# Graph attention on one core: forward maxima kept in PSUM, column numbers in bf16 beside the sums, and a new place for ScalarE's comparison

## The chip, the cores and the metric

The kernel runs on 1 core of a Trainium2 chip. The engines of the core are TensorE (PE; its weight loads are shown as PEld), VectorE (DVE), ScalarE (ACT), GpSimd (POOL) and SyncE (SP). Each runs its own queue of instructions in order and waits for the others by semaphores. The metric is the device time of the whole kernel in microseconds (us); lower is better. Several runs are taken and their median is given. One further execution is recorded by the profiler, and all durations of single instructions come from it.

## The reference

A graph has 6250 nodes with 128 features and 200,000 edges, sorted by their destination `dst`. After a layer norm and a ReLU come two edge convolutions and one attention layer. Only the attention is touched by the change:

```python
q = (h @ qw + qb).reshape(n, H, HD)          # H = 8 heads of HD = 16
k = (h @ kw + kb).reshape(n, H, HD)
v = (h @ vw + vb).reshape(n, H, HD)
logits = (q[dst] * k[src]).sum(-1) * scale + (edge_attr @ ew + eb)
amax = jax.ops.segment_max(logits, dst, num_segments=n)
pe = jnp.exp(logits - amax[dst])
ssum = jax.ops.segment_sum(pe, dst, num_segments=n)
w = pe / jnp.clip(ssum[dst], 1e-06)
o = jax.ops.segment_sum(w[:, :, None] * v[src], dst, num_segments=n)
```

The convolutions ahead of it gather rows of `src` in the same way, put them through a small network for each edge and sum by `dst`.

## The kernel before

**Tiling.** The edges are cut into 196 chunks of 1024 (NT = 8 columns of 128 edges). As they are sorted by destination, a chunk's destinations nearly always lie in a narrow window of nodes, and its sums go to two neighbouring blocks of 128 nodes of a table in SBUF (`flat`). What does not fit into a window is done later in loops (`leftovers`, `left`, `left_rows`).

**Stages.** `conv(1)`, `conv(2)` and the attention each run `pipeline`, which writes out the instructions step by step: step n fetches chunk n + 2 (GpSimd gathers its rows from memory in eight indirect DMAs, L618; SyncE loads the rest), computes the first half for chunk n and the second half for some earlier chunk. `in_order` then fixes this written order for VectorE, ScalarE, TensorE and SyncE. So where a line stands in `pipeline` decides where it stands in its engine's queue. GpSimd's gathers wait for free buffers.

**One step of the attention, in the order of the code.**

- `compared` (L613, L614; ScalarE): turns the relative destinations of chunk n + 2 into a matrix of zeros and ones, `ohT`, by a square and a ReLU. It works in place on 112 x 1024 values.
- `second`, for a chunk k about nine steps old, whose maxima are known: `onehot` (L624, VectorE) compares the column numbers `iota` with each edge's destination to give `oh`; `add_late` (L1261 to L1267, VectorE) adds the rescaled sums of chunk k-2 to the table; `weighted` has ScalarE fill a column of `v` with the weights `pe` (L1234) and VectorE multiply the gathered values by them (L1235); ScalarE fills two more pieces of `v` (L1340, L1341); `sums` (L1242, TensorE) multiplies `oh` by `v` in eight accumulating products (two passes each, so 16 in the profile) into a PSUM tile `u`; `merge_late` (L1275, L1278, L1249 to L1257) takes the maxima of chunk k-1 from its `u`, compares them with those kept so far (VectorE) and computes two rescaling factors by exponentials, `al` (L1255, written back into `u`) and `be` (L1257) (ScalarE).
- `first`, that is `logits`, for chunk n: VectorE multiplies the products `qe` by the gathered keys in two pieces (L1178: banks 0 and 1 of `qe`, then bank 2), ScalarE copies the edge terms `ebs` out of `qe` after each (L1179), and VectorE reduces and adds (L1181, L1183).
- `products` (L1169, TensorE) makes `qe` for chunk n + 1.
- One piece of a batch of finished nodes (`attention_nodes`).

**Maxima by runs.** For a run of up to eight chunks, `maxima` finds the maximum of each destination. TensorE transposes the logits `lg` into PSUM, so that 64 rows (8 chunks x 8 heads) hold the 1024 edges in order, in two halves of 512, which share one PSUM buffer (tag `blk`). VectorE scans each half forward into `fw` in SBUF (L1210), and then scans `fw` backward in place (L1213); `nbs` and `nbe` reset the maximum where a destination begins and ends. TensorE transposes the result back into `rm`. There are 23 runs of eight and then runs of 6, 4 and 2. `maxima` is a generator whose pieces are woven into `second`.

**PSUM.** Eight banks of 512 f32 per partition: `iota` one, `blk` one (also used by the node batches), `qe` three, `pe` one, and `u` two, one for each of two rotating buffers. The tile framework sets the semaphore waits from what each instruction reads and writes.

Of the kernel before, what the change touches and what calls it, by code (L numbers as in the profile page):

```python
# [8 lines left out]
FP = mybir.dt.float32  # L9
BF = mybir.dt.bfloat16  # L10
I32 = mybir.dt.int32
AF = mybir.ActivationFunctionType
ALU = mybir.AluOpType
# [8 lines left out]
P = 128  # L22
D = 128
H = 8
HD = 16
NT = 8
CH = NT * P
G = 8
# [16 lines left out]
def kernel(ctx: ExitStack, tc: tile.TileContext, x, src, dst, eat, w, out):  # L45
# [621 lines left out]
                nc.sync.dma_start(out=k.ea, in_=eat[:, bass.ds(c * CH, CH)])  # L667
                body(k)

    def left_rows(k, pools, rows_d, tag, shape, bufs):  # L670

        lp = pools["left"]
        k.rows = lp.tile([P, DB], FP, name="l_rows")
        nc.vector.memset(k.rows[:, D:], 0.0)
        nc.sync.dma_start(out=k.rows[:, :D], in_=rows_d[bass.ds(k.win * P, P), :])
        onehot(k, pools, iota_j)
        k.ohf = lp.tile([P, NT, P], FP, name="l_ohf")
        per = shape[1]
        for a in range(0, NT, per):
            n = min(per, NT - a)  # L680
            tp = pools["ps"].tile(shape, FP, name="l_tp", tag=tag, bufs=bufs)
            for t in range(n):
                nc.tensor.transpose(tp[:, t, :P], k.oh[:, a + t, :], ident)
            nc.scalar.copy(k.ohf[:, a:a + n, :], tp[:, :n, :P])
# [13 lines left out]
    def pipeline(i, stage, aside=iter(())):  # L698

        start = len(nc.cur_bb.bb.instructions)
        ends, todo = steps_of(i)
        starts = {n: j for j, (n, _) in enumerate(plans[i])}
        ahead = stage.ahead
        ks, under_way = {}, []
        for c in range(ahead):  # L710
            ks[c] = stage.fetch(c)
            compared(ks[c])
        stage.products(ks[0])
        for n, seconds in enumerate(todo):
            if n + ahead < NCH:
                ks[n + ahead] = stage.fetch(n + ahead)
            if n + 1 < NCH and stage.soon:
                stage.products(ks[n + 1])
            run = [ks[c] for c in ends.get(n, ())]
            stage.root(run)  # L720
            if n + ahead < NCH:
                compared(ks[n + ahead])
            stage.second(run, [ks.pop(c) for c in seconds])
            if n < NCH:
                stage.first(ks[n])
            stage.finish()
            if n + 1 < NCH and not stage.soon:
                stage.products(ks[n + 1])
            if n + 1 < len(todo) and todo[n + 1]:
                stage.early(ks[todo[n + 1][0]])  # L730
            if n in starts:
                for _ in aside:
                    pass
                under_way.append(stage.batch(starts[n]))
            for g in list(under_way):
                if next(g, STOP) is STOP:
                    under_way.remove(g)
            if n > 4:
                next(aside, None)
            if n < NCH:  # L740
                stage.reduce(ks[n])
        stage.flush()
        for g in (*under_way, aside):
            for _ in g:
                pass
        in_order(start)
# [205 lines left out]
    def conv(i):  # L952
# [4 lines left out]
        with ExitStack() as es:  # L957
# [154 lines left out]
            nc.sync.dma_start(out=wcl, in_=wc_d[i])  # L1112

            def left(k):
                left_rows(k, pools, a_d[i], "m", [P, NT, D], 2)
                k.g = gp.tile([P, NT, D], FP, name="g")
                gather(k, k.g, b_d[i])
                k.h = hs[0]
                hidden(k, [(k.ohf.rearrange("p t e -> p (t e)"), k.rows[:, :D]), (k.ea, wcl)])
                var = vp.tile([P, NV + BN * H], FP, name="var")  # L1120
                first(k, var, 0)()
                nc.vector.reciprocal(rs_ps[:, :NT * H], deviations(NT * H, var)[:, :NT * H])
                k.rs = rs_ps[:, :NT * H]
                normed(k)
                summed(k)
                s = U[:, bass.ds(k.win, 1), :wide].rearrange("p o c -> p (o c)")
                nc.vector.tensor_tensor(s, s, k.u[:, 0, :wide], ALU.add)
# [23 lines left out]
    with ExitStack() as es:  # L1151
# [1 line left out]
        pools = {"oh": pool("oh", 2), "ps": pool("ps", 1, space=PSUM)}  # L1153
        gp, wk, vp = pool("gp", G + 3), pool("wk", 2), pool("vp", 1)
        ps_ = pools["ps"]
        iota = ps_.tile([P, D], FP, name="iota")
        nc.vector.tensor_copy(iota, iota_j)
        nodes = Nodes(np_of(pool("np", 1)), lambda: ps_.tile([P, BN, D], FP, name="nd", tag="blk"))

        TB = 3  # L1160
        WHOLE = NT // TB
# [34 lines left out]
        def maxima(run, lg, nb, bp):  # L1196

            n, c0 = len(run), run[0].c  # L1200
            q = n * H
            fw = bp.tile([G * H, CH], FP, name="fw")
            half = CH // 2
            for a in range(2):
                lt = ps_.tile([G * H, 4, P], FP, name="lt", tag="blk")
                for t in range(4):
                    nc.tensor.transpose(lt[:q, t, :], lg[:, 4 * a + t, :n, :].rearrange("p c h -> p (c h)"), ident)
                yield
                at = slice(a * half, (a + 1) * half)
                nc.vector.tensor_tensor_scan(  # L1210
                    fw[:q, at], nb["nbs"][:q, at], lt[:q].rearrange("p t e -> p (t e)"),
                    fw[:q, half - 1:half] if a else -BIG, ALU.add, ALU.max)
            nc.vector.tensor_tensor_scan(  # L1213
                fw[:q, ::-1], nb["nbe"][:q, ::-1], fw[:q, ::-1], -BIG, ALU.add, ALU.max)
            rm = ps_.tile([P, NT, G, H], FP, name="rm", tag="blk")
            for t in range(NT):
                nc.tensor.transpose(rm[:, t, :n, :].rearrange("p c h -> p (c h)"), fw[:q, t * P:(t + 1) * P], ident[:q, :q])
            yield
            wl = vp.tile([P, NT, G, H], FP, name="wl")
            e3 = ef[:, c0 * NT:(c0 + n) * NT].rearrange("p (c t) -> p t c", t=NT)  # L1220
            nc.vector.tensor_tensor(lg[:, :, :n, :], lg[:, :, :n, :], rm[:, :, :n, :], ALU.subtract)
            pe = ps_.tile([P, NT, G, H], FP, name="pe", tag="pe")
            nc.scalar.activation(pe[:, :, :n, :], lg[:, :, :n, :], AF.Exp)
            for t in range(NT):
                nc.vector.tensor_tensor(
                    wl[:, t, :n, :], rm[:, t, :n, :], e3[:, t, :, None].to_broadcast([P, n, H]), ALU.mult)
            for j, k in enumerate(run):
                k.pe, k.wl = pe[:, :, j, :], wl[:, :, j, :]
# [8 lines left out]
                k.pe[:, :, :, None].to_broadcast([P, NT, H, HD]), ALU.mult)  # L1237

        def sums(k, wide):
            k.u = ps_.tile([P, 512], FP, name="u", tag="u", bufs=2)  # L1240
            for t in range(NT):
                nc.tensor.matmul(k.u[:, :wide], lhsT=k.oh[:, t, :], rhs=k.v[:, t, :wide],  # L1242
                                 start=(t == 0), stop=(t == NT - 1))

        def merge(k, m, tt, cm, n):


            mn = wk.tile([P, n, H], FP, name="mn")
            nc.vector.tensor_tensor(mn, cm, m, ALU.max)  # L1249
            d = wk.tile([P, 2, n, H], FP, name="d")  # L1250
            nc.vector.tensor_tensor(d[:, 0], m, mn, ALU.subtract)
            nc.vector.tensor_tensor(d[:, 1], cm, mn, ALU.subtract)  # L1252
            nc.vector.tensor_copy(m, mn)
            k.al = k.u[:, 160:160 + n * H].rearrange("p (q h) -> p q h", h=H)
            nc.scalar.activation(k.al, d[:, 0], AF.Exp)  # L1255
            k.be = wk.tile([P, n, H], FP, name="be")
            nc.scalar.activation(k.be, d[:, 1], AF.Exp)  # L1257

        def add(k, tt, n):
            tt = tt.rearrange("p q (h c) -> p q h c", c=HD + 1)  # L1260
            nc.vector.tensor_tensor(tt, tt, k.al[:, :, :, None].to_broadcast([P, n, H, HD + 1]), ALU.mult)  # L1261
            up = k.u[:, 192:192 + n * VK].rearrange("p (q h c) -> p q h c", h=H, c=HD + 1)
            u = k.u[:, :VK].rearrange("p (h c) -> p h c", c=HD + 1)
            for q in range(n):
                nc.vector.tensor_tensor(
                    up[:, q], u, k.be[:, q, :, None].to_broadcast([P, H, HD + 1]), ALU.mult)
            nc.vector.tensor_tensor(tt, tt, up, ALU.add)  # L1267
# [17 lines left out]
        class Stage:  # L1285
# [34 lines left out]
            def second(self, run, ks):  # L1320
# [6 lines left out]
                for n, k in enumerate(ks):  # L1327
                    mine = pieces if n == len(ks) - 1 else iter(())
                    next(mine, None)
                    onehot(k, pools, iota)  # L1330
                    if self.sums:
                        self.sums[0].win = value(w0_i, self.sums[0].c, DVE, NW - 1)
                    next(mine, None)
# [37 lines left out]

        def left(k):
            lp = pools["left"]
            left_rows(k, pools, a_d[3], "blk", [P, BN, P], 1)
            k.g = gp.tile([P, NT, KV], FP, name="g")
            gather(k, k.g, kv_d)
            products(k, [(k.ohf.rearrange("p t e -> p (t e)"), k.rows), (k.ea, webl)])
# [5 lines left out]
            for a in range(2):  # L1383
                nc.vector.tensor_scalar(neg, k.ohf[:, 4 * a:4 * a + 4, :], 1.0, BIG, ALU.subtract, ALU.mult)
                for h in range(H):
                    bc = ps_.tile([P, 4, P], FP, name="l_bc", tag="blk")
                    for t in range(4):
                        nc.tensor.transpose(bc[:, t, :], lg[:, 4 * a + t, h:h + 1].to_broadcast([P, P]), ident)
                    nc.vector.tensor_tensor_reduce(
# [59 lines left out]
```

## Time and profile before

| | |
|---|---|
| time, median of 3 runs | 6209.37 us (6209.28 to 6218.48) |
| the profiled execution | 6216.17 us, of which the span of instructions is 6214.2 us |
| VectorE busy | 5103.6 us (82%) |
| GpSimd busy | 4541.8 us (73%) |
| TensorE matmuls busy | 3590.1 us (58%) |
| ScalarE busy | 3301.8 us (53%) |
| TensorE's granted clock, mean | 0.769 |

The two convolutions take the first 4,100 us or so (the first gather of the attention starts at 4110.62 us), the attention and its last nodes the rest. In a row of a group stand the line, the engine, the operation, the output and the inputs, the shape and the count; then the busy time in us and the mean in ns; then the idle time of the engine just before these instructions, and which instruction or transfer ended it. In a timeline row stand the start, the duration, the engine and the line, and in brackets the idle time ahead. The durations of neighbours on one engine may overlap by some hundredths of a microsecond. GpSimd's 0.30 us between two gathers is its time for issuing and not a wait for others. The names of tiles come without their numbers. The clock is the share of the full rate that TensorE was granted: a busy TensorE at a low clock works more slowly.

### The profile page before, as it was taken

Reading aid. Unit: us, or ns where it says so; the run is one execution under the profiler, and the core shown is the slowest. Engines: PE = TensorE matmul, PEld = TensorE weight load, DVE = VectorE, ACT = ScalarE, POOL = GpSimd, SP = SyncE. Lnnn points to the kernel's source line nnn. Section 1 sums busy time; section 2 is a strip of 40 time slices with the busy share of each in tenths; the row PEclk is TensorE's granted clock in tenths of the full one; section 3 lists DMA queues with packets and bytes.
Section 4 is the critical chain, followed back from the end, with each engine's and each line's share of the span. In section 5 each row is a group of like instructions: output and inputs, shape, how many; then the busy total and the mean of one; then the engine's idle time right before and its main releaser. Section 6 shows DMA issues by size and latency. Waiting matters only on the chain. (4 is left out here: it accounts for less than half of the span.)

```text
span 6214.2 us, 71765 instructions
## 1 busy us (share of the span) xinstructions
PE 3590.1 (58%) x20957; PEld 3411.2 (55%) x20958; DVE 5103.6 (82%) x7368; ACT 3301.8 (53%) x5097; POOL 4541.8 (73%) x4718
## 2 busy tenths in 40 slices
PE   4555555555555455555655565645665566565655
PEld 4555555555555455555655555635555555555554
DVE  6878888888888677877888888847788888888888
ACT  5666666666666566666666666633333333333332
POOL 5777777777777577777777777757777777777773
PEclk8777777777877777777787778767777877887787
DMA  6544444444444344444444444445666666666653
GB/s 166 127 111 110 102 125 111 108 115 114 109 114 108 88 108 108 104 107 109 116 113 122 122 121 118 113 116 157 162 163 167 169 167 164 172 171 165 171 160 75
DMA packets 414303, 800.30 MB, mean 129 GB/s; under 512 B 101813, under 2 KB 274984, under 8 KB 379496
## 3 DMA queue, kind: packets, MB, share of 16 engines
q0 software_dynamic: 175616, 411.34, 27.4%
q1 hardware_dynamic: 232646, 380.69, 22.3%
q10 hardware_dynamic: 5632, 3.51, 0.2%
q8 instruction: 172, 2.82, 0.2%
q14 instruction: 237, 1.94, 0.1%
HBM read 754.19 MB, written 40.96 MB: 128 GB/s over the span
## 5 line engine op out<-in xcount | busy, mean ns | idle before, releaser
L618 POOL DMA_INDIRECT g<-b_d,src_i x3136 | 2989.4, 953 | 972.0 <-issue 899.2
L1018 PE MATMUL u<-h,oh 128*128 128x129 f32 (+1 forms) x6272 | 1249.8, 380 | 1459.2 <-ACT h L1013 1459.2
L1018 PEld LDWEIGHTS u<-h,oh 128*128 128x128 f32 x6272 | 1152.4, 284 | 1538.5 <-ACT h L1013 1533.2
L618 POOL DMA_INDIRECT g<-kv_d,src_i x1568 | 1531.9, 977 | 497.2 <-issue 440.1
L988 PE MATMUL m<-pk,ohT 117*128 117x128 f32 x6272 | 939.4, 313 | 211.7 <-DVE h L994 170.1
L988 PEld LDWEIGHTS m<-pk,ohT 117*128 117x128 f32 x6272 | 906.5, 230 | 234.2 <-DVE h L994 190.7
L1242 PE MATMUL u<-v,oh 128*128 128x145 f32 x3136 | 672.2, 392 | 552.6 <-DVE nm L1275 550.6
L1242 PEld LDWEIGHTS u<-v,oh 128*128 128x128 f32 x3136 | 624.4, 279 | 587.4 <-issue 587.4
L994 DVE TENSOR_TENSOR h<-m,g 128x1024 f32<-128x1024 f32 x392 | 477.2, 1217 | 543.1 <-DMA g<-b_d,src_i 538.9
L1013 ACT ACTIVATE h<-h 128x1024 f32<-128x1024 f32 x392 | 414.1, 1056 | 623.1 <-DVE h L1012 607.1
L996 ACT ACTIVATE sq<-h 128x1024 f32<-128x1024 f32 x392 | 412.8, 1053 | 548.1 <-DVE h L994 547.3
L613 ACT ACTIVATE ohT<-ohT,minus_p 112x1024 f32<-112x1024 f32 x588 | 669.5, 1139 | 43.6 <-DMA ohT<-rel_d 43.5
L614 ACT ACTIVATE ohT<-ohT 112x1024 f32<-112x1024 f32 x588 | 621.4, 1057 | 18.6
L1169 PE MATMUL qe<-pk,ohT 117*128 117x136 f32 x3136 | 489.2, 319 | 146.0 <-ACT ebs L1179 141.1
L1169 PEld LDWEIGHTS qe<-pk,ohT 117*128 117x128 f32 x3136 | 470.0, 228 | 164.4 <-ACT ebs L1179 159.2
L997 DVE TENSOR_REDUCE var<-sq 128x64 f32<-128x1024 f32 x392 | 476.1, 1215 | 67.3 <-ACT sq L996 67.0
L1011 DVE TENSOR_TENSOR h<-h,cps 128x1024 f32<-128x1024 f32 x392 | 478.4, 1220 | 13.5
L1012 DVE TENSOR_TENSOR h<-h,cps 128x1024 f32<-128x1024 f32 x392 | 478.4, 1220 | 13.4
L624 DVE TENSOR_TENSOR oh<-cps,dm 128x1024 f32<-128x1024 f32 x392 | 475.4, 1213 | 0.2
L1008 DVE TENSOR_TENSOR h<-h,cps 128x1024 f32<-128x1024 f32 x392 | 475.2, 1212 | 0.0
L1178 DVE TENSOR_TENSOR g<-qe,g 128x768 f32<-128x768 f32 (+1 forms) x392 | 270.8, 691 | 213.9 <-DMA g<-kv_d,src_i 136.7
L1255 ACT ACTIVATE u<-d 128x16 f32<-128x16 f32 x196 | 36.7, 187 | 760.7 <-DVE d L1252 700.7
(264 smaller groups left out, 4272.4 us busy)
## 6 DMA issues: line engine op xcount, KB each, us to landing
ohT<-rel_d SPq DMA_DIRECT2D x294, 896.0 KB
g<-b_d,src_i POOLq DMA_INDIRECT x3136
pk<-a_d SPq DMA_DIRECT2D x588, 56.0 KB
g<-kv_d,src_i POOLq DMA_INDIRECT x1568
ohT<-in_eat_dram SPq DMA_DIRECT2D x294, 40.0 KB
a_d<-n_o SPq DMA_DIRECT2D x28, 256.0 KB
kv_d<-n_o SPq DMA_DIRECT2D x28, 256.0 KB
n_h<-h_d SPq DMA_DIRECT2D x19, 256.0 KB
```

The lines of the kernel that those rows point to most:

```text
L613: nc.scalar.activation(k.ohT[:WN, :], k.ohT[:WN, :], AF.Square, bias=minus_p[:WN])
L614: nc.scalar.activation(k.ohT[:WN, :], k.ohT[:WN, :], AF.Relu, bias=1.0, scale=-4.0)
L618: nc.gpsimd.indirect_dma_start(out=g[:, t, :table_d.shape[1]], out_offset=None, in_=table_d, in_offset=bass.IndirectOffsetOnAxis(ap=k.src[ ...
L624: return nc.vector.tensor_tensor(k.oh, iota[:, None, :].to_broadcast([P, NT, P]), k.dm[:, :, None].to_broadcast([P, NT, P]), ALU.is_equal)
L988: nc.tensor.matmul(k.m[:, t, :], lhsT=lhs[:, t * P:(t + 1) * P], rhs=rhs, start=(j == 0), stop=(j == len(terms) - 1))
L994: nc.vector.tensor_tensor(k.mt, k.m, k.g, ALU.add)
L997: return lambda: nc.vector.tensor_reduce(var[:, j * NT * H:(j + 1) * NT * H], sq.rearrange("p t (g c) -> p (t g) c", c=HD), AX.X, ALU.add)
L1011: nc.vector.tensor_tensor(k.mt, k.mt, over_edges(gam), ALU.mult)
L1012: nc.vector.tensor_tensor(k.mt, k.mt, over_edges(bet), ALU.add)
L1018: nc.tensor.matmul(k.u[:, 0, :wide], lhsT=k.oh[:, t, :], rhs=k.h[:, t, :wide], start=(t == 0), stop=(t == NT - 1))
L1169: nc.tensor.matmul(k.qe[:, t // TB, at:at + DB], lhsT=lhs[:, t * P:(t + 1) * P], rhs=rhs, start=(j == 0), stop=(j == len(terms) - 1))
L1242: nc.tensor.matmul(k.u[:, :wide], lhsT=k.oh[:, t, :], rhs=k.v[:, t, :wide], start=(t == 0), stop=(t == NT - 1))
```

## The change

- Forward maxima. Eight transposes fill one tile of two banks (`blk`, now two banks wide, still one buffer). One forward scan over 1024 columns works in place in PSUM, and the backward scan reads PSUM and writes `fw`. The pieces of the generator are cut in the same places, but both scans now stand in the last one.
- Sums and column numbers. One PSUM tile `us` of two banks takes the place of the rotating `u` and of `iota`. Chunk k uses bank k.c % 2. The column numbers, as bf16, lie at the end of each of the two banks (viewed as f32 when they are written there), and `onehot` reads the copy in the chunk's own bank. `al` and the product `up` move to new columns.
- Comparison. In the attention alone (`soon` is False there), `compared` now stands behind `second`, so that ScalarE fills `v` and computes the merge's exponentials first. In the convolutions its place is the same.
- `left_rows` takes its PSUM tiles from the node batches' `bank`, in pieces of four.

```diff
-    def left_rows(k, pools, rows_d, tag, shape, bufs):
+    def left_rows(k, pools, rows_d, bank):
...
-        per = shape[1]
-        for a in range(0, NT, per):
-            n = min(per, NT - a)
-            tp = pools["ps"].tile(shape, FP, name="l_tp", tag=tag, bufs=bufs)
+        for a in range(0, NT, BN):
+            n = min(BN, NT - a)
+            tp = bank()
...
             stage.root(run)
-            if n + ahead < NCH:
+            if n + ahead < NCH and stage.soon:
                 compared(ks[n + ahead])
             stage.second(run, [ks.pop(c) for c in seconds])
+            if n + ahead < NCH and not stage.soon:
+                compared(ks[n + ahead])
             if n < NCH:
                 stage.first(ks[n])
...
-        iota = ps_.tile([P, D], FP, name="iota")
-        nc.vector.tensor_copy(iota, iota_j)
-        nodes = Nodes(np_of(pool("np", 1)), lambda: ps_.tile([P, BN, D], FP, name="nd", tag="blk"))
+        us = ps_.tile([P, 2, 512], FP, name="us")
+        AL, UP, IO = VK + H + 1, VK + 3 * H + 1, 3 * VK + 3 * H + 1
+        iota_b = wk.tile([P, D], BF, name="iota_b")
+        nc.vector.tensor_copy(iota_b, iota_j)
+        for j in range(2):
+            nc.vector.tensor_copy(us[:, j, IO:IO + D // 2], iota_b.bitcast(FP))
+
+        def iota_of(k):
+            return us[:, k.c % 2, IO:IO + D // 2].bitcast(BF)
+
+        def banks():
+            return ps_.tile([P, 2, 512], FP, name="blk", tag="blk")
+
+        def bank():
+            return banks()[:, 0, :].rearrange("p (t e) -> p t e", e=P)
+
+        nodes = Nodes(np_of(pool("np", 1)), bank)
...
             fw = bp.tile([G * H, CH], FP, name="fw")
-            half = CH // 2
+            lt = banks().rearrange("p a c -> p (a c)")[:q, :CH]
             for a in range(2):
-                lt = ps_.tile([G * H, 4, P], FP, name="lt", tag="blk")
-                for t in range(4):
-                    nc.tensor.transpose(lt[:q, t, :], lg[:, 4 * a + t, :n, :].rearrange("p c h -> p (c h)"), ident)
+                for t in range(4 * a, 4 * a + 4):
+                    nc.tensor.transpose(
+                        lt[:, t * P:(t + 1) * P], lg[:, t, :n, :].rearrange("p c h -> p (c h)"), ident)
                 yield
-                at = slice(a * half, (a + 1) * half)
-                nc.vector.tensor_tensor_scan(
-                    fw[:q, at], nb["nbs"][:q, at], lt[:q].rearrange("p t e -> p (t e)"),
-                    fw[:q, half - 1:half] if a else -BIG, ALU.add, ALU.max)
+            nc.vector.tensor_tensor_scan(lt, nb["nbs"][:q], lt, -BIG, ALU.add, ALU.max)
             nc.vector.tensor_tensor_scan(
-                fw[:q, ::-1], nb["nbe"][:q, ::-1], fw[:q, ::-1], -BIG, ALU.add, ALU.max)
-            rm = ps_.tile([P, NT, G, H], FP, name="rm", tag="blk")
+                fw[:q, ::-1], nb["nbe"][:q, ::-1], lt[:, ::-1], -BIG, ALU.add, ALU.max)
+            rm = banks()[:, 0, :].rearrange("p (t g h) -> p t g h", t=NT, g=G)
...
         def sums(k, wide):
-            k.u = ps_.tile([P, 512], FP, name="u", tag="u", bufs=2)
+            k.u = us[:, k.c % 2, :]
...
-            k.al = k.u[:, 160:160 + n * H].rearrange("p (q h) -> p q h", h=H)
+            k.al = k.u[:, AL:AL + n * H].rearrange("p (q h) -> p q h", h=H)
...
-            up = k.u[:, 192:192 + n * VK].rearrange("p (q h c) -> p q h c", h=H, c=HD + 1)
+            up = k.u[:, UP:UP + n * VK].rearrange("p (q h c) -> p q h c", h=H, c=HD + 1)
...
-                    onehot(k, pools, iota)
+                    onehot(k, pools, iota_of(k))
```

In the changed kernel the lines of the attention lie 12 to 15 lower: `nm` (L1275) is L1287 there, the fill of `v` (L1234) L1246, the sums (L1242) L1254, the logit products (L1169) L1184, the multiplication by keys (L1178) L1193 and the copy of `ebs` (L1179) L1194.

## The prediction

> **What bounds the kernel now.** I read the page's shares first, then the third stage by its groups and waits, then one step of it in the timeline. Only the third (attention) stage is touched, from about 4,110 us on; the two stages before it keep every instruction, so I cost nothing there.
>
> Groups of the third stage, 4,300 to 6,100 us (busy us, mean ns | idle before, releaser):
>
> ```profile
> L618 POOL DMA_INDIRECT g<-kv_d,src_i x1404 | 1372.8, 978 | 427.9 <-issue 392.3 <-DMA g<-kv_d,src_i 7.3 <-DVE flat L1261 7.0
> L1242 PE MATMUL u<-v,oh 128*128 128x145 f32 x2835 | 608.9, 392 | 514.1 <-DVE nm L1275 513.4
> L624 DVE TENSOR_TENSOR oh<-iota,dm 128x1024 f32<-128x1024 f32 x177 | 215.1, 1215 | 0.2 <-issue 0.2
> L1235 DVE TENSOR_TENSOR v<-g,pe 128x1024 f32<-128x1024 f32 x177 | 214.4, 1211 | 47.2 <-ACT v L1234 47.2
> L1178 DVE TENSOR_TENSOR g<-qe,g 128x256 f32<-128x256 f32 x174 | 73.9, 425 | 103.4 <-DMA g<-kv_d,src_i 59.5 <-ACT ebs L1179 43.9
> L1213 DVE TENSOR_TENSOR_SCAN fw<-nbe,fw 64x1024 f32<-64x1024 bf16 x21 | 48.0, 2284 | 0.7
> L1275 DVE SCALAR_TENSOR_TENSOR nm<-u,nm 128x2 f32<-128x2 f32 x177 | 26.5, 150 | 0.0
> ```
>
> The reader should see three things. The gathers (L618) run almost without a break: eight per chunk, starting every 1.255 us (5057.44, 5058.70, ... 5062.46 in the timeline), so a chunk cannot take less than 10.04 us. 1404 x 1.255 = 1762 of these 1800 us. VectorE (DVE) is the second limit: 1535 of 1800 us busy, and its waits are small. And L1275, the first VectorE instruction that reads a chunk's sums, has 0.0 idle before it: it reads the sums of the chunk before, which TensorE finished long ago.
>
> One step of the timeline:
>
> ```profile
> 5057.61 1.21 DVE L1235 TENSOR_TENSOR v<-g,pe 128x1024 f32<-128x1024 f32 x1
> ...
> 5058.75 0.15 DVE L1275 SCALAR_TENSOR_TENSOR nm<-u,nm 128x2 f32<-128x2 f32 x1
> ...
> 5058.97 4.20 PE L1242 MATMUL u<-v,oh 128*128 128x145 f32 x16 [5.55 <-DVE nm L1275]
> ...
> 5059.74 0.20 ACT L1257 ACTIVATE be<-d 128x16 f32<-128x16 f32 x1
> 5059.86 0.96 DVE L1178 TENSOR_TENSOR g<-qe,g 128x768 f32<-128x768 f32 x1
> ...
> 5060.85 0.20 ACT L1179 COPY ebs<-qe 128x48 f32<-128x48 f32 x1 [0.92 <-DVE g L1178]
> 5061.08 0.42 DVE L1178 TENSOR_TENSOR g<-qe,g 128x256 f32<-128x256 f32 x1 [0.27 <-ACT ebs L1179]
> ...
> 5061.61 1.15 ACT L613 ACTIVATE ohT<-ohT,minus_p 112x1024 f32<-112x1024 f32 x1
> ```
>
> TensorE sums chunk k (4.20 us) while VectorE is already merging chunk k-1 and multiplying logits: that overlap is what the change touches. Note also the 0.27 us: the second L1178 reads bank 2 of `qe`, the first `ebs` copy reads banks 0 and 1, and yet one waits for the other. Accesses to one PSUM tile are put in order as a tile, not by bank.
>
> **The change part by part.** The sum is made against the profiled execution, 6216.2 us (7 us above the median of 6209.4).
>
> *Sums and column numbers in one tile `us`.* Two tiles `u`, which rotated, become the halves of one tile, chosen by k.c % 2. By the rule just seen, reading half (k-1) % 2 must wait for a write to half k % 2. The built program bears it out: L1275 (now L1287) waits for a TensorE count that is reached only with the sums of chunk k, issued just ahead of it; before, that count was reached with chunk k-1, 16 lower. So 195 times VectorE stops behind L1235 until TensorE has summed the chunk. Behind L1287 stand the rest of the merge, both logit products, the reduction and the next one-hot; ScalarE's two exponentials, its comparison and `ebs` wait for the merge in turn, and TensorE's next logit products for `ebs`. Price: TensorE starts 0.22 us after L1275's old place (5058.97 - 5058.75), takes 608.9/177 = 3.44 us a chunk, and releases its reader in about 0.04 us. So 3.70 us x 195 = +721 us. Bounds: groups of 16 last from 2.22 us (4263.55) to 4.20 us, so +484 to +870. I take the mean, because the new step has the spacing of places where both occur: the logit products after over 3 us of idleness, then the sums 1.2 to 1.6 us later:
>
> ```profile
> 4340.57 3.65 PE L1169 MATMUL qe<-pk,ohT 117*128 117x136 f32 x16 [3.49 <-ACT ebs L1179]
> 4345.81 2.22 PE L1242 MATMUL u<-v,oh 128*128 128x145 f32 x16 [1.59 <-DVE nm L1275]
> ...
> 4423.28 3.99 PE L1169 MATMUL qe<-pk,ohT 117*128 117x136 f32 x16 [5.55 <-ACT ebs L1179]
> 4428.52 4.14 PE L1242 MATMUL u<-v,oh 128*128 128x145 f32 x16 [1.24 <-DVE nm L1275]
> ```
>
> The Trainium skill ("TensorE: Matmul & The Clock Gate", section "Part 1: The HAM clock gate") says that TensorE falls to half rate after an idle window of about 3.4 us and needs a busy one of that length to come back. The rows agree on the fall; on the return they go both ways. By the rule alone a run of 4 us seldom fills a whole free-running window, most sums would be slow, and the sum would come out near the slow rival below.
>
> *Comparison (L613, L614) moved behind the fills and the merge's exponentials.* It now stands between `be` (L1257) and the first `ebs` copy. `be` starts at 5059.74, the next ScalarE instruction could start 0.13 later; L613 to L614 is 1.19 us and L614 to its successor 0.96, so `ebs` would start at 5062.02 in place of 5060.85: the second L1178 comes 1.17 us later. From step 9 to 193 that is 185 x 1.17 = +216 us. In 18 steps a table load of 1.28 us precedes the exponentials; the first L1178 hid most of it (0.52 idle at 5050.62 in place of 0.27), now the longer ScalarE chain shows it: about 1.0 more, +18. The fills, now first, no longer hold up L1235: 47.2 us of waits for 177 chunks go, -52 for 196. Bounds for the whole edit: 0 to -52 for the last term, nothing for the others, which are spacings.
>
> *Waits for gathers.* With a longer step the gathers end early: the 64.7 us at L1178 (59.5 and 5.2 at its two forms) go: -65.
>
> *Scans.* Two halves (1206 and 1266 ns) and a backward scan (2284) become two full ones with PSUM sources. 1206 ns read PSUM for 512 elements, so 1024 cost about 2.28 to 2.41; 26 x (4.56 to 4.82 against 4.76) is -5 to +2, taken as 0. The first half's wait for its transposes (11.2 + 2.3 here, about 17 in the stage) goes. In its place the full scan waits for all eight, which stand behind logit products of up to 4.0 us: these start 0.22 us after L1181, the eight take 1.2 to 2.1, and the scan is due 4.1 us after L1181, so 1.3 to 2.2 us x 26 = 34 to 57. Net +17 to +40, taken as +25.
>
> *Column numbers in bf16.* L624 keeps its shape. No row has two bf16 inputs and an f32 output; the nearest is L624 itself (one bf16 input, 1215 ns), and I take it: 0. The fastest VectorE rate per element is L313's cast, 964 ns for 1568: that would be 0.63 us, -115 in all. The other end is a small loss of a few us. The Trainium skill ("VectorE: DVE Perf Modes", section "What auto-detection actually checks") allows a doubled two-input rate only where every tensor is 16-bit; the output here is f32.
>
> *Left loops, node batches, memory.* The loops for leftovers show no instruction in the trace. Node batches use the same single `blk` buffer, now two banks wide. Gathers and SyncE's queue keep their order. 0.
>
> Sum: 721 + 216 + 18 - 52 - 65 + 25 = +863, so 7079 for a profiled execution and 7072 for a median.
>
> **The rivals.**
> - *TensorE always at one rate.* All sums at 2.22 us: 195 x 1.22 = 238 less, 6834. All at 4.20: 148 more, 7220. For either: both lengths occur at the new spacing.
> - *The halves stay independent.* The wait is for chunk k-1 after all: 721 less, 6351, still slower through the comparison. For it: the code chooses alternating halves. Against: `qe` above, and the built count.
> - *One-hot at a doubled rate.* 115 less, 6957. Only L313, with one input, speaks for it.
> - *The other side: the gathers absorb it.* If VectorE's new waits fell into time in which it would wait for gathers (at L1178) or fills, the step would stay at the gathers' pace: at best 38 us per 1800, 41 in the stage, are saved, 6168. This decides while the new waits stay under (64.7 + 47.2)/177 = 0.63 us a chunk. I have 3.70 + 1.17, and the shortest sums alone are 2.22.
>
> **How the numbers follow.** Forecast 0.74, sums all fast 0.07, all slow 0.08, one-hot 0.03, independent halves 0.05, gathers absorb 0.03. The likeliest gives 7072. The range takes in the clock's bounds (6834 to 7220) with some 30 us of the smaller terms: 6800 to 7240; outside lie independent halves, gathers, and combinations. Differences within 0.2% are about what a measurement of this kernel cannot tell from no change. Only the gather rival is faster, 0.03; 0.01 for a tie on its way; slower 0.96.
>
> **What the profile after would show.** Right: idle before `nm` near 3.7 us a chunk, released by TensorE's sums; the second L1178 idle about 1.4 us for `ebs`; none for fills at L1235; gathers pausing some 4 us a chunk, released by VectorE; L624 still near 1215 ns. The forecast is wrong if `nm` shows no idle time, if TensorE's sums settle at one rate, or if the stage's steps stay near 10.2 us.

## The result and the profile after

The changed kernel takes 7110.75 us (median of 5 runs, 7106.77 to 7112.2), against 6209.37 us for the kernel before in 5 runs beside it (6204.23 to 6218.48). The ratio is 1.1445, with a 95% interval of 1.1432 to 1.1458: it is slower by 14%.

First the place of the loss. The windows view gives, for one stretch of time, its length, then the busy time (and count) of PE, PEld, DVE, ACT and POOL, the granted clock, the DMA share and GB/s. The attention stage of the kernel before:

```profile
4110.00:6214.00 2104.00, 1229.55 (x6943) 1158.69 (x6943) 1724.56 (x3689) 712.33 (x1891) 1531.89 (x1568) 0.77 0.60 159
```

The same stage of the changed kernel:

```profile
4110.00:7110.00 3000.00, 1588.76 (x6935) 1470.11 (x6934) 1739.89 (x3663) 699.93 (x1891) 1479.57 (x1566) 0.64 0.39 111
```

The stage grew by 896 us. What lies ahead of it did not change: VectorE is busy for 3379.0 us of the first 4110 us in one kernel and 3380.1 us in the other. VectorE's busy time in the stage grew by only 15 us and GpSimd's fell, so the stage did not get more work; it got waits. TensorE is busy for 359 us more with the same products, while the clock that it was granted fell from 0.77 to 0.64.

The costliest groups of the changed kernel's page (busy us, mean ns, then the idle time ahead and what ended it):

```profile
L618 POOL DMA_INDIRECT g<-kv_d,src_i x1568 | 1482.4, 945 | 1376.6 <-DVE v L1247 933.1
...
L1184 PE MATMUL qe<-pk,ohT 117*128 117x136 f32 x3136 | 767.1, 438 | 853.2 <-ACT ebs L1194 848.3
...
L1254 PE MATMUL us<-v,oh 128*128 128x145 f32 x3136 | 719.6, 412 | 405.7 <-DVE v L1247 404.8
...
L1287 DVE SCALAR_TENSOR_TENSOR nm<-us,nm 128x2 f32<-128x2 f32 x196 | 31.3, 160 | 755.0 <-PE us L1254 755.0
```

L1287 answers L1275 of before, which had no idle time at all: it now stands idle for 755.0 us, released by TensorE's sums. The gathers, which set the pace before, now pause for 933.1 us until VectorE has read the buffers of an older chunk.

VectorE's waits in the stage (from 4105 us on), summed by what it waited for: us in total, times, the longest. Of the changed kernel:

```profile
DVE nm L1287 <- PE us L1254: 755.0, 195, 4.4
DVE g L1193 <- ACT ebs L1194: 278.1, 189, 2.7
DVE g L1193 <- DMA g<-kv_d,src_i: 63.8, 18, 13.8
DVE v L1247 <- ACT v L1246: 23.8, 18, 1.7
```

The same list of the kernel before:

```profile
DVE g L1178 <- DMA g<-kv_d,src_i: 136.7, 52, 13.5
DVE v L1235 <- ACT v L1234: 51.2, 22, 3.7
DVE g L1178 <- ACT ebs L1179: 47.4, 157, 0.5
```

The wait for sums appears 195 times, once a chunk, and the wait for `ebs` has grown to nearly six times its size. One step of the changed kernel in the timeline shows both:

```profile
5301.60 1.22 DVE L1247 TENSOR_TENSOR v<-g,pe 128x1024 f32<-128x1024 f32 x1
...
5302.96 4.21 PE L1254 MATMUL us<-v,oh 128*128 128x145 f32 x16 [2.57 <-DVE v L1247]
...
5307.21 0.16 DVE L1287 SCALAR_TENSOR_TENSOR nm<-us,nm 128x2 f32<-128x2 f32 x1 [4.39 <-PE us L1254]
...
5308.21 0.20 ACT L1269 ACTIVATE be<-d 128x16 f32<-128x16 f32 x1
5308.30 0.96 DVE L1193 TENSOR_TENSOR g<-qe,g 128x768 f32<-128x768 f32 x1
5308.31 1.13 ACT L613 ACTIVATE ohT<-ohT,minus_p 112x1024 f32<-112x1024 f32 x1
...
5309.48 1.06 ACT L614 ACTIVATE ohT<-ohT 112x1024 f32<-112x1024 f32 x1
5310.44 0.18 ACT L1194 COPY ebs<-qe 128x48 f32<-128x48 f32 x1
...
5310.65 0.42 DVE L1193 TENSOR_TENSOR g<-qe,g 128x256 f32<-128x256 f32 x1 [1.40 <-ACT ebs L1194]
...
5311.34 3.99 PE L1184 MATMUL qe<-pk,ohT 117*128 117x136 f32 x16 [4.17 <-ACT ebs L1194]
...
5318.20 3.24 PE L1254 MATMUL us<-v,oh 128*128 128x145 f32 x16 [2.88 <-DVE v L1247]
```

TensorE sums chunk k from 5302.96 to 5307.17 while VectorE stands still for 4.39 us, though `nm` reads the sums of chunk k-1 in the other bank. Then the comparison (L613, L614) holds the first copy of `ebs`, and VectorE stands still again, for 1.40 us. While VectorE merges, TensorE has nothing to do. Step and step alternate where they overlapped before.

### The profile page after: what moved, and what is told of

It reads as the page before. It is cut to its first block, busy times and chain, and to the rows that moved or that the text cites. A ratio compares the mean times of both kernels' runs of the same rounds, so it can differ in the third digit from the quotient of the medians.

```text
span 7110.4 us, 71712 instructions
## 1 busy us (share of the span) xinstructions
PE 3950.0 (56%) x20957; PEld 3723.9 (52%) x20958; DVE 5120.0 (72%) x7344; ACT 3288.5 (46%) x5097; POOL 4487.6 (63%) x4718
## 5 line engine op out<-in xcount | busy, mean ns | idle before, releaser
L618 POOL DMA_INDIRECT g<-kv_d,src_i x1568 | 1482.4, 945 | 1376.6 <-DVE v L1247 933.1
L1184 PE MATMUL qe<-pk,ohT 117*128 117x136 f32 x3136 | 767.1, 438 | 853.2 <-ACT ebs L1194 848.3
L1184 PEld LDWEIGHTS qe<-pk,ohT 117*128 117x128 f32 x3136 | 708.7, 329 | 909.8 <-ACT ebs L1194 904.7
L1254 PE MATMUL us<-v,oh 128*128 128x145 f32 x3136 | 719.6, 412 | 405.7 <-DVE v L1247 404.8
L1254 PEld LDWEIGHTS us<-v,oh 128*128 128x128 f32 x3136 | 669.3, 296 | 452.7 <-issue 452.7
L995 DVE TENSOR_TENSOR h<-m,g 128x1024 f32<-128x1024 f32 x392 | 477.2, 1217 | 550.2 <-DMA g<-b_d,src_i 528.7
L1267 ACT ACTIVATE us<-d 128x16 f32<-128x16 f32 x196 | 36.7, 187 | 1791.5 <-DVE d L1264 1758.9
L613 ACT ACTIVATE ohT<-ohT,minus_p 112x1024 f32<-112x1024 f32 x588 | 667.2, 1135 | 34.9 <-DMA ohT<-rel_d 26.3
L614 ACT ACTIVATE ohT<-ohT 112x1024 f32<-112x1024 f32 x588 | 621.2, 1057 | 18.6
L1287 DVE SCALAR_TENSOR_TENSOR nm<-us,nm 128x2 f32<-128x2 f32 x196 | 31.3, 160 | 755.0 <-PE us L1254 755.0
L1193 DVE TENSOR_TENSOR g<-qe,g 128x768 f32<-128x768 f32 (+1 forms) x392 | 271.0, 691 | 366.3 <-ACT ebs L1194 278.1
L1012 DVE TENSOR_TENSOR h<-h,cps 128x1024 f32<-128x1024 f32 x392 | 478.5, 1221 | 13.4
L1013 DVE TENSOR_TENSOR h<-h,cps 128x1024 f32<-128x1024 f32 x392 | 478.4, 1220 | 13.4
```

The costliest lines, as they stand in the source:

```text
L613: nc.scalar.activation(k.ohT[:WN, :], k.ohT[:WN, :], AF.Square, bias=minus_p[:WN])
L614: nc.scalar.activation(k.ohT[:WN, :], k.ohT[:WN, :], AF.Relu, bias=1.0, scale=-4.0)
L618: nc.gpsimd.indirect_dma_start(out=g[:, t, :table_d.shape[1]], out_offset=None, in_=table_d, in_offset=bass.IndirectOffsetOnAxis(ap=k.src[ ...
L995: nc.vector.tensor_tensor(k.mt, k.m, k.g, ALU.add)
L1012: nc.vector.tensor_tensor(k.mt, k.mt, over_edges(gam), ALU.mult)
L1013: nc.vector.tensor_tensor(k.mt, k.mt, over_edges(bet), ALU.add)
```

## The experiments

The theory: nearly all of the loss is two waits, one from making the two halves of `us` one tile, one from the place of the comparison, and everything else is small. The rivals: the scans, the bf16 column numbers or the clock carry a part of it; or the place of the comparison is to be blamed for more than its own wait.

### Four kernels on a chip that was slow for every kernel

Two tiles in place of one (changed kernel):

```diff
-        us = ps_.tile([P, 2, 512], FP, name="us")
+        us = [ps_.tile([P, 512], FP, name=f"us{j}") for j in range(2)]
...
-            nc.vector.tensor_copy(us[:, j, IO:IO + D // 2], iota_b.bitcast(FP))
+            nc.vector.tensor_copy(us[j][:, IO:IO + D // 2], iota_b.bitcast(FP))
...
-            return us[:, k.c % 2, IO:IO + D // 2].bitcast(BF)
+            return us[k.c % 2][:, IO:IO + D // 2].bitcast(BF)
...
-            k.u = us[:, k.c % 2, :]
+            k.u = us[k.c % 2]
```

> The changed kernel (7110.75 us) with one edit: the two halves of `us` are two PSUM tiles of one bank each, so that reading chunk k-1's sums no longer has to be ordered behind the write of chunk k's. Theory (the tile as a whole is put in order): the 755.0 us of idle time before `nm` and the 14 us of lost overlap go, the comparison's 231 us stay: 6300 to 6380 us. Rival 1 (the column numbers in the banks of the sums, or the scans in PSUM, slow the work by their place): banks and contents are the same as in the changed kernel, so it stays within 1% of 7110. Rival 2 (most of the loss is the comparison's new place): over 6900.

The comparison back in its old place (changed kernel, one tile kept):

```diff
-            if n + ahead < NCH and stage.soon:
+            if n + ahead < NCH:
                 compared(ks[n + ahead])
             stage.second(run, [ks.pop(c) for c in seconds])
-            if n + ahead < NCH and not stage.soon:
-                compared(ks[n + ahead])
```

> The changed kernel with one edit: the comparison stands ahead of the second half again, as before the change; one tile `us` stays. Theory: the wait for `ebs` at the second multiplication by keys falls from 278 to about 47 us, the waits for the fills of `v` rise by some 30: 6870 to 6950 us. Rival (the comparison's place is hidden behind the wait for the sums): 7050 to 7110.

Both of these edits together:

> The changed kernel with both edits: two tiles, and the comparison in its old place. What is left of the change are the full scans in PSUM, the bf16 column numbers and the common banks. Theory: these are worth next to nothing, 6190 to 6225 us, within 0.3% of the kernel before. Rival (a double rate for the one-hot, or scans that cost more in PSUM): over 0.5% away from it.

And the kernel before with the comparison alone moved behind `second`:

```diff
-            if n + ahead < NCH:
+            if n + ahead < NCH and stage.soon:
                 compared(ks[n + ahead])
             stage.second(run, [ks.pop(c) for c in seconds])
+            if n + ahead < NCH and not stage.soon:
+                compared(ks[n + ahead])
```

> The kernel before with one part of the change: the comparison behind the second half. Theory: wait for `ebs` +231 us, waits for fills -27, waits for gathers -73, which leaves +131: 6310 to 6370 us, the same as the changed kernel with two tiles. Rival (the gathers' pace hides it): within 0.5% of 6209.

Measured: 8030.03, 8007.14, 8009.33 and 8037.79 us, beside 8017.37 us (7972.84 to 8057.92) for the kernel before on this chip. The ratios are 1.002, 0.9983, 0.9984 and 1.0032. No theory expected that the kernel before itself would take 1800 us longer. VectorE's longest waits here were ones whose releaser the profile doesn't see (`remote`), already in the two convolutions, which no edit touches. From the waits of the kernel with both edits:

```profile
DVE h L993 <- remote: 909.8, 150, 34.3
```

Beside waits of up to 34.3 us one of 4 need not show in the time. These runs say nothing on the theories, and the cause of the pauses stays open. All kernels below ran on chips on which the kernel before took 6211.77 or 6216.57 us; the first, third and fourth edit were repeated there, the second was not.

### The one tile alone

The kernel before, with nothing changed but the sums' tile (`k.c = 0` serves the loops for leftovers):

```diff
+        us = ps_.tile([P, 2, 512], FP, name="us")
...
-            k.u = ps_.tile([P, 512], FP, name="u", tag="u", bufs=2)
+            k.u = us[:, k.c % 2, :]
```

> The kernel before with one part of the change: the rotating tiles `u` become the halves of one tile `us`; column numbers, scans and comparison as before. Theory: idle time before `nm` of about 755 us appears, 14 us of overlap go, 73 us of waits for gathers go: 6860 to 6950 us. Rival (it takes the column numbers in the same banks too): within 1% of 6209.

Measured: 6932.76 us against 6211.77, a ratio of 1.1162 (1.1145 to 1.1179), or +721 us. VectorE's waits in the stage:

```profile
DVE nm L1276 <- PE us L1243: 755.9, 195, 4.4
DVE g L1179 <- DMA g<-kv_d,src_i: 64.2, 21, 13.7
DVE v L1236 <- ACT v L1235: 60.9, 21, 3.8
DVE g L1179 <- ACT ebs L1180: 54.6, 187, 0.6
```

The first line is the changed kernel's within a microsecond, and the second shows the gathers' waits halved, as there. `ebs` and the fills stay near the values of before. So this part alone makes the whole wait for sums.

### Two tiles in the changed kernel

The first edit above, repeated.

> The changed kernel with the halves of `us` as two PSUM tiles of one bank each, once more, on a chip on which the kernel before takes its usual 6210 us. Theory (a tile is put in order as a whole): the idle time before `nm` goes to 0, the comparison's cost stays: 6310 to 6380 us, as for the changed kernel with the merge written first (6354.13). Rival 1 (contents of the banks): within 1% of 7110. Rival 2 (the comparison is the greater part): over 6900.

Measured: 6309.51 us against 6216.57, a ratio of 1.0149 (1.0134 to 1.0165), half a microsecond below the theory's 6310 to 6380. VectorE's groups in the stage:

```profile
L1193 DVE TENSOR_TENSOR g<-qe,g 128x256 f32<-128x256 f32 x196 | 83.2, 425 | 292.6 <-ACT ebs L1194 237.0 <-DMA g<-kv_d,src_i 55.6
L1287 DVE SCALAR_TENSOR_TENSOR nm<-us,nm 128x2 f32<-128x2 f32 x196 | 29.7, 151 | 1.1 <-PE us L1254 1.1
```

Each half still has a bank of its own, with the same contents, products and readers as in the changed kernel; only the tile that it is declared in differs. The wait for sums falls from 755.0 to 1.1 us, and 801 us of the time go. What is left is the wait for `ebs`.

### The place of the comparison alone

The fourth edit above, repeated.

> The kernel before with the comparison behind the second half and nothing else, once more. Theory: waits for `ebs` of 235 to 280 us in place of 47 appear at the second multiplication by keys, the waits for fills and gathers fall: 6310 to 6370 us. Rival (the gathers' pace hides it): within 0.5% of 6210.

Measured: 6320.02 us, a ratio of 1.0162 (1.0146 to 1.0177), or +103 us. From VectorE's groups in the stage:

```profile
L1180 DVE TENSOR_TENSOR g<-qe,g 128x256 f32<-128x256 f32 x196 | 83.3, 425 | 289.5 <-ACT ebs L1181 237.1 <-DMA g<-kv_d,src_i 51.1 <-ACT ohT L614 1.4
```

The wait for `ebs` goes from 47.4 to 237.1 us, and that for the fills from 51.2 to 2.4. The move does what it says (ScalarE fills `v` in time), and pays four times as much for it at `ebs`: +190 against -49. With the waits for gathers, which fall from 136.7 to 105.6 us, that makes +110, near the +103 of the time.

### Both undone: the scans and the column numbers that are left

> The changed kernel with two tiles and the comparison in its old place, once more: the full scans in PSUM, the bf16 column numbers and the shared banks alone. Theory: within 0.3% of the kernel before, 6190 to 6225 us. Rival (the gain of the kernel with the comparison behind `ebs`, 6172.66, comes from the scans or the column numbers): 6165 to 6185.

Measured: 6182.44 us, a ratio of 0.9943 (0.9929 to 0.9956). The theory's 6190 to 6225 missed; the rival's 6165 to 6185 holds. So the rest of the change, which the prediction took for a loss of 25 us, is a gain of some 34 us.

### Two tiles, and the comparison behind `first`

```diff
             stage.second(run, [ks.pop(c) for c in seconds])
-            if n + ahead < NCH and not stage.soon:
-                compared(ks[n + ahead])
             if n < NCH:
                 stage.first(ks[n])
+            if n + ahead < NCH and not stage.soon:
+                compared(ks[n + ahead])
```

> The changed kernel with two tiles, and the comparison behind the copies of `ebs` (after the first half), so that it stands neither ahead of the fills nor ahead of `ebs`. Theory: the wait for `ebs` is that of before (about 47 us), the waits for fills are those after the change (24 in place of 51), and the gathers' pace allows at most 41 us less than before: 6165 to 6205 us. Rival (the gathers alone set the time): 6205 to 6215, no gain.

Measured: 6172.66 us against 6211.77, a ratio of 0.9941 (0.9928 to 0.9955). It is the fastest kernel here. VectorE waits 9.1 us for fills and 49.3 us for `ebs`, so this place hurts neither. But the waits for gathers rise to 151.6 us. I had put the gain down to the place.

### That place alone, in the kernel before

```diff
-            if n + ahead < NCH:
+            if n + ahead < NCH and stage.soon:
                 compared(ks[n + ahead])
...
                 stage.first(ks[n])
+            if n + ahead < NCH and not stage.soon:
+                compared(ks[n + ahead])
```

> The kernel before with one edit, which the change does not have: the comparison stands behind the copies of `ebs`. Theory: the gain of the changed kernel with two tiles and this place (6172.66) is that of the place alone: 6165 to 6190 us. Rival (it needs the scans in PSUM or the bf16 column numbers): 6200 to 6215.

Measured: 6212.64 us, a ratio of 0.9993 (0.9984 to 1.0002). The theory's 6165 to 6190 missed. The waits for fills fall from 51.2 to 9.9 us and come back as waits for gathers (136.7 to 161.9) and for the scans' transposes (18.3 to 34.3): the gathers set the pace, and a wait of VectorE that is taken away is only moved. So the gain of the two kernels before this one has to come from faster gathers. The gathers in the stage, as duration in ns (shortest, median, longest), of the kernel before:

```profile
L618 POOL DMA_INDIRECT g<-kv_d,src_i x1568: 942/947/2976, 4110.6 to 6119.2; - x196
```

and of the changed kernel with both edits undone:

```profile
L618 POOL DMA_INDIRECT g<-kv_d,src_i x1568: 942/946/1454, 4108.5 to 6078.6; - x196
```

In the kernel before, and in the one with only this place changed, 24 gathers take over 1.6 us (59.1 and 57.6 us together), and each of them runs beside a backward scan; in the two faster kernels none takes so long. 24 gathers at the usual 0.95 us would take 22.8 us, so these cost 36 us, of a total that falls by 38.7 us (1531.9 to 1493.2) and of a gain of 34 us in time. Where they stand, the timeline of the kernel before shows:

```profile
5026.15 2.28 DVE L1213 TENSOR_TENSOR_SCAN fw<-nbe,fw 64x1024 f32<-64x1024 bf16 x1
5026.62 2.58 POOL L618 DMA_INDIRECT g<-kv_d,src_i  x1 [0.30 <-issue]
...
5029.50 0.95 POOL L618 DMA_INDIRECT g<-kv_d,src_i  x1 [0.30 <-issue]
```

and the same place with both edits undone, where the scan reads PSUM:

```profile
5006.97 0.94 POOL L618 DMA_INDIRECT g<-kv_d,src_i  x1 [0.30 <-issue]
5007.16 2.28 DVE L1223 TENSOR_TENSOR_SCAN fw<-nbe,blk 64x1024 f32<-64x1024 bf16 x1
5008.22 0.95 POOL L618 DMA_INDIRECT g<-kv_d,src_i  x1 [0.30 <-issue]
```

Beside the backward scan whose inputs are both in SBUF a gather takes 2.58 us; beside the same scan with one input in PSUM it takes 0.95. The rows show this side by side; a kernel before with only that input moved was not run, so the scan was not tried apart from the rest of the change, the bf16 column numbers among it. What speaks against those: `onehot` takes 1215 ns before and 1217 ns in this kernel, and the gain goes with the number of long gathers while `onehot` runs 196 times in every kernel. With the comparison behind `first`, 24 long gathers go and the ratio falls from 0.9993 to 0.9941, some 32 us. With the comparison behind `second`, the kernel before (6320.02 us) has only 7 long gathers, worth some 12 us, and the changed kernel with two tiles (6309.51 us), which has none, is only 10.5 us faster; the intervals of these two overlap, but 34 us lie outside them.

### The merge written ahead of the sums

```diff
-                    sums(k, VK + H + 1)
                     if self.sums:
                         merge_late(self.sums[0])
                         self.late.append(self.sums.pop())
+                    sums(k, VK + H + 1)
```

> The changed kernel with one edit: the merge of chunk k-1 is written ahead of the sums of chunk k, one tile `us` stays. Theory (order within the tile): the read no longer follows the write, VectorE goes on at once and TensorE waits for the merge instead, which nobody misses: 6300 to 6400 us. Rival (a tile of two banks costs its time wherever the merge stands): near 7110.

Measured: 6354.13 us, a ratio of 1.023 (1.0214 to 1.0245). VectorE's row and TensorE's row in the stage:

```profile
L1287 DVE SCALAR_TENSOR_TENSOR nm<-us,nm 128x2 f32<-128x2 f32 x196 | 29.6, 151 | 0.0
...
L1254 PE MATMUL us<-v,oh 128*128 128x145 f32 x3136 | 739.5, 420 | 717.0 <-ACT us L1267 716.8 <-DVE v L1247 0.3
```

The one tile still puts the two halves in order, but now in the other direction: TensorE waits 716.8 us for ScalarE to write `al` of the chunk before into its half. Nearly all of it is off VectorE's chain, and the time is only some 45 us over that of the kernel with two tiles (6354.13 - 6309.51, on two chips). VectorE does still wait for sums at `onehot`, whose column numbers lie in the same tile (us in total, times, the longest):

```profile
DVE oh L624 <- PE us L1254: 34.8, 8, 5.7
```

The wait belongs to the tile; its price belongs to which of the two is written first.

### The sums made twice

The eight sum products are issued a second time, over the first, so that the values are the same and TensorE has twice the work there:

```diff
+            for t in range(NT):
+                nc.tensor.matmul(k.u[:, :wide], lhsT=k.oh[:, t, :], rhs=k.v[:, t, :wide],
+                                 start=(t == 0), stop=(t == NT - 1))
```

> The changed kernel with the sums of every chunk computed twice in a row into the same place, the second time over the first. Theory (VectorE stands still for as long as TensorE sums): the second pass adds 2.2 to 4.2 us for each of 195 chunks, +430 to +820 us: 7540 to 7930. Rival (the wait before `nm` has another cause than TensorE's work): within 1% of 7110.

Measured: 7465.59 us, a ratio of 1.2017 (1.1995 to 1.2039), or +355 us over the changed kernel. VectorE's row:

```profile
L1290 DVE SCALAR_TENSOR_TENSOR nm<-us,nm 128x2 f32<-128x2 f32 x196 | 31.3, 160 | 1118.3 <-PE us L1257 1112.4 <-issue 5.9
```

The wait for sums grew by 357 us and the time by 355: what TensorE takes there is on the path in full. The size lies under the 430 to 820 us that I gave. The second pass takes 2.32 us in the mean (455.6 us in all) and under 2.7 us in 169 of 196 chunks, the first pass fell from 719.6 to 667.2 us, and the records of the two overlap a little: from the start of the first to the end of the second they take 1087 us, 367 more than the single pass.

## Why the prediction was right

The prediction was 7072 us, the range 6800 to 7240; the time is 7110.75. By its own steps:

- **Sums in one tile: +721 forecast, +769 measured** (755.0 us of waits, and 14 of the 15 us by which VectorE's busy time grew: the records of neighbours overlap by some 0.07 us, and across an idle gap they can't, 195 times). The mechanism is shown twice, by making it alone (755.9) and by taking it away (1.1). The mis-sized term of the sum is TensorE's 3.44 us a chunk: it took 719.6/196 = 3.67. The sums came out between the mean of before and the slow bound of 4.20: short and long ones go on occurring, but in other shares. Over 3.7 us took 109 of 196 before and 129 now, under 2.7 us 57 and 36. That both lengths occur at the new spacing was right, but it gave no reason why their shares should stay as before. The rival with all sums slow was off by 109 us, the forecast by 39.
- **Place of the comparison: +216 +18 forecast, +231 measured** (47.4 to 278.1 at `ebs`). The spacing in the timeline is the one worked out: `be`, 0.10 us, L613, L614, `ebs`, and 1.40 us of idle time.
- **Fills: -52 forecast, -27 measured** (51.2 to 23.8). In the kernel before, the move alone takes 49 of the 51 us. In the changed kernel 18 places are left, at which ScalarE stands in a copy of a node batch (L765) that waits for TensorE; TensorE's slower logit products (438 ns, 315 in the kernel with the merge first) are ahead of it. With two tiles and the comparison in the same place only 2.5 us of waits for fills are left, so they come with the one tile; the reason given was read from rows and not tested.
- **Gathers: -65 forecast, -73 measured** (136.7 to 63.8).
- **Scans' wait for their transposes: +25 forecast, 0 measured.** VectorE waited 20.6 us at the scans before (18.3 and 2.3) and waits 20.6 us now (11.9 and 8.7). The order was the one assumed (logit products, eight transposes, scan), but the term was over-sized: 1.3 to 2.2 us at each of 26 scans were forecast, and 15 of them wait, for 1.4 us in the mean. At 4998.79 the scan has no wait at all, behind logit products of 3.19 us in place of 4.0. The scans' durations in all fell by 5 us (4756 to 4564 ns, 26 times), the end that I gave as -5.
- **Column numbers: 0 forecast, 0 measured.** The rows of the changed kernel's stage:

```profile
L624 DVE TENSOR_TENSOR oh<-us,dm 128x1024 f32<-128x1024 bf16 x196 | 238.7, 1218 | 2.1 <-ACT us L1267 1.1 <-issue 0.3
...
L1224 DVE TENSOR_TENSOR_SCAN blk<-nbs,blk 64x1024 f32<-64x1024 bf16 x23 | 52.6, 2286 | 17.2 <-DMA pk<-a_d 8.7 <-PE blk L1221 7.5
L1225 DVE TENSOR_TENSOR_SCAN fw<-nbe,blk 64x1024 f32<-64x1024 bf16 x23 | 52.4, 2278 | 0.8
```

The measured terms sum to 769 + 231 - 27 - 73 + 0 - 5 = 895, against 896 us by which the stage grew. The forecast's +863 is 33 short: 48 in TensorE's sums and 25 in the fills, against 25 in the scans' wait, 8 in the gathers and a few in the smaller terms. That errors of both signs bring the 73 us of the first two down to 33 is luck. The other 6 us of the 39 are the 7 us that I took off because the profiled execution of before lay above its median; that of the changed kernel does not.

What the prediction missed altogether has no part in the time: that gathers beside the backward scan are held. It read that the gathers "run almost without a break" and took the two scans as 0, and both hid 24 long gathers in a mean of 977 ns. In the changed kernel the gathers wait for VectorE anyway, and being freed there gains nothing; without the two waits it accounts for the whole gain of the rest of the change.

The rival of independent halves falls with the run that makes the one tile alone. The gather rival falls because 3.9 + 1.2 us a chunk are far over the 0.63 us that gathers could cover; its pace holds for the kernels with two tiles and the comparison in its old place or behind `first`, where a chunk's gathers start 10.06 and 10.05 us after those of the chunk before, in the mean (10.25 in the kernel before).

## What to carry to other kernels

Two buffers that are used in turn, one read while the other is written, are better two tiles: here the halves of one tile were put in order against each other, and that alone cost 721 of 901 us with no instruction added. Where they have to share a tile, what is written first decides who waits. Before an instruction is moved in an engine's queue, look at what stands behind the new place as well as at what stands behind the old one: the comparison freed 49 us of fills and held up `ebs` by 190 us, and a place two lines further on held up neither. Where one engine sets the pace, look at its rows by longest and shortest and not by mean, for the gain may lie in what another engine does to it.

## What the runs showed of the hardware that I had not expected

- **A scan on VectorE holds a gather of GpSimd.** With both inputs of the backward scan in SBUF the gather beside it took 2.58 us in place of 0.95, with one input in PSUM it took 0.95; the scan took 2.28 us in both. All 24 gathers of over 1.6 us in the kernel before run beside that scan, and no gather that runs for more than 0.3 us beside a scan that reads PSUM takes over 0.96 us, in that kernel or in the changed one with both edits undone. The Trainium skill ("GPSIMD Engine Reference", section "1. Specifications") says that GpSimd shares its way into SBUF with VectorE and that the two get in each other's way where VectorE reads two inputs from SBUF. The trace agrees, and shows that a gather's instruction on GpSimd counts among what is held.
- **TensorE's return to its full rate goes both ways.** After 4 us of idle time the logit products ran slowly (3.99 us at 5311.34), and the sums that follow took 2.22 us at 5225.83, 3.24 at 5318.20 and 4.21 at 5302.96, 3.67 in the mean. The second pass, where the sums were made twice, was faster (2.32 us in the mean). By the rule of the Trainium skill that the prediction weighed ("TensorE: Matmul & The Clock Gate", section "Part 1: The HAM clock gate"), most sums would be slow. The trace agrees for most of them, 129 of 196 over 3.7 us, but 36 took under 2.7 us, and the mean of 3.67 stayed under the slow bound of 4.20.
